# Placing a batch's exponentials behind every chunk of layers 1 to 3, and stretching the pacing sum from 1150 to 1195

## The chip, the cores and the metric

The kernel runs on one core of a Trainium2 chip. The metric is the device time of one execution in microseconds (us). Five executions of the kernel before gave 10002.39, 10005.69, 10021.45, 10026.64 and 10043.83 us, so the median is 10021.45 us.

## The reference, cut to what matters

The input x is (4, 64, 64, 128) in float32: four independent batches of 4096 tokens with 128 channels. Four layers follow one another, each with residual additions.

```python
# layer 0: deformable attention. 4 groups g of 32 channels, 9 sampled points, 4 bilinear corners
qkv = depthwise3x3(gn(x) @ w_qkv + b_qkv) + b_dw
off[g] = conv1x1(pconv(q, pconv_off_w[g]), w_off[g]);  mask = sigmoid(conv1x1(pconv(q, ...)))
ks, vs = bilinear samples of k and v at 9 moved points, times mask     # a gather by data
attn = softmax(q . ks over the 9 points)
x = x + (sum(attn * vs) @ w_proj + b_proj)
# layer 1: linear attention (softmax of q over channels, of k over tokens), then a norm
x = x + norm(linear_attention(gn(x)))
# layer 2: t = t + q * sum(k * v); then 64 experts, each picks its 8 best tokens
t = t + q * (k * v).sum(tokens)
pooled = top-8 tokens of each expert, weighted by the router's softmax over the tokens
t = t + scatter(gelu(pooled @ w1[e] + b1) @ w2[e] + b2)
# layer 3: causal linear attention, then 16 spectral filters (long causal convolutions)
t = t + causal_linear_attention(ln(t))
t = t + sum_k (filter_k * u) @ M_k (plus and minus) + autoregressive part   # u = ln(t)
```

## The kernel before, in words

**Two streams.** The kernel is written as one program in which the function `hybrid` interleaves two streams. While layer 0's attention of batch b runs, layers 1 to 3 of batch b - 1 run beside it; beside batch 0 the tables of the filters are prepared instead (`prepare`, with its own pacing sum `SETUP`). The last batch's layers 1 to 3 have nothing beside them and run at the end with more buffers (`wide`).

**Layer 0's attention.** A batch has 8 chunks c, each with 4 tiles t of 128 tokens, each with 4 groups g: 128 groups. `Layer0.attend` (L591) issues one group and then yields. A group is nine indirect gathers on POOL into the tile gt (L604), each of 128 rows; VectorE's products and sums pr, s, s times weights, sc and mx (L613 to L623); one exponential ex on ScalarE (L626), which is two instructions in the trace; then VectorE's qa (L630), pv (L635) and o (L638). gt has three buffers, so that the gathers of a group wait for pv of the third group before it; pr and pv have one buffer each. Beside it `front(b + 1)` computes layer 0's projections for the next batch during the first 15 of the batch's 32 tiles.

**Layers 1 to 3.** `Post.run` is a generator called `behind`. It yields after each small step, and gives with the yield a number that stands for the step's time. In order: layer 1; layer 2's attention; the router (8 chunks, then the pooling of the chosen tokens), the experts in 16 steps of four experts, the scatter in 8 steps; layer 3's attention; the tokens and the autoregressive part; the filters' front, 128 filter cycles of 4.7 each, and an end stage of 20. An expert step loads its weights on SyncE's queue (w1 and w2, three buffers each), multiplies on PE into ph (L1106), copies hs on ScalarE, transposes on PE into pt (L1115), adds a bias on VectorE (g, L1120), applies Gelu on ScalarE and multiplies on PE into po (L1126). A filter cycle is `convolve` (eight matmuls, 16 in the trace, from the table th and the spectrum xh into pq, L1397, and two copies y on ScalarE, L1411) and `mix` (eight matmuls, 16 in the trace, from the cycle before's y into pa, L1422); `put` writes four finished rows. The words "the end stage" and "layer 0's last rows" in what follows mean the last 20 units of the filters and `end`, which projects a chunk and writes it out.

**Pacing.** After each group `hybrid` takes steps from `behind` until their numbers sum to `total * (groups done) / 128`, where total is `WORK` = 1150. The steps taken after one group are called that group's chunk here. The numbers of layers 1 to 3 sum to 1209.6 before the change and after it, so that with 1150 some steps are left when the 128 groups are issued; they follow the last group, before the next batch's first.

**Order on each engine.** The program's order isn't the order on the engines. A scheduler places each instruction on its engine by the time at which it expects its inputs, and instructions of the two streams overtake each other. `tc.issue_after(ins)` fixes one such relation: what is issued within it stands behind `ins` on its engine. The class `Turns` keeps such marks. Before the change, an exponential stands behind the last copy y of the filters' cycles issued so far (`after("filters")`), and a copy y stands behind the last exponential issued so far (`after("samples")`). The mark "filters" is removed at the end of each batch, so that in layers 1 to 3 ahead of the filters only the scheduler decides.

Of the kernel before, what the change touches and what calls it, by code (L numbers as in the profile page):

```python
# [56 lines left out]
class Turns:  # L57


    def __init__(self, tc):  # L60
        self.tc = tc
        self.last = {}

    def after(self, who):

        ins = self.last.get(who)
        return nullcontext() if ins is None else self.tc.issue_after(ins)

    def took(self, who):
        self.last[who] = next(  # L70
            i for i in reversed(self.tc.nc.cur_bb.bb.instructions)
            if i.engine == mybir.EngineType.Activation
        )


def make_consts(tc, ctx):
# [97 lines left out]
class Layer0:  # L174
# [416 lines left out]
    def attend(self, b, c, t):  # L591

        nc = self.nc
        blk = self.blk[b, c]
        o = blk.o

        qa = blk.qa[t // 2]
        q0 = t % 2 * C
        den = self.sm.tile([P, G], F32, tag="den", name="den")
        for g in range(G):  # L600
            gt = self.gp.tile([P, K2, 256], F32, tag="gt", name="gt")
            for i in range(K2):
                col = g * K2 + i
                nc.gpsimd.indirect_dma_start(  # L604
                    out=gt[:, i, :], out_offset=None, in_=self.tbl[b % 2][:, :],
                    in_offset=bass.IndirectOffsetOnAxis(
                        ap=blk.idx[:, t, col : col + 1], axis=0
                    ),
                )
            corners = gt.rearrange("p i (c s) -> p (i c) s", c=4)  # L610
            cw = blk.cw[:, t, g * K2 : (g + 1) * K2, :]
            pr = self.t1.tile([P, 4 * K2, 32], F32, tag="pr", name="pr")
            nc.vector.tensor_mul(  # L613
                pr, corners[:, :, 0:32],
                qa[:, q0 + 32 * g : q0 + 32 * g + 32].unsqueeze(1).to_broadcast([P, 4 * K2, 32]),
            )
            s4 = self.sm.tile([P, 4 * K2], F32, tag="s4", name="s4")
            nc.vector.tensor_reduce(s4, pr, AX.X, ALU.add)  # L618
            nc.vector.tensor_mul(s4, s4, cw.rearrange("p i c -> p (i c)"))
            sc = self.sm.tile([P, K2], F32, tag="sc", name="sc")  # L620
            nc.vector.tensor_reduce(sc, s4.rearrange("p (i c) -> p i c", c=4), AX.X, ALU.add)
            mx = self.sm.tile([P, 1], F32, tag="mx", name="mx")
            nc.vector.tensor_reduce(mx, sc, AX.X, ALU.max, negate=True)  # L623
            ex = self.sm.tile([P, K2], F32, tag="ex", name="ex")
            with self.turns.after("filters"):
                nc.scalar.activation(ex, sc, AF.Exp, bias=mx, accum_out=den[:, g : g + 1])  # L626
            self.turns.took("samples")
            a0 = 2 * C + g % 2 * 4 * K2
            aw = qa[:, a0 : a0 + 4 * K2]
            nc.vector.tensor_mul(  # L630
                aw.rearrange("p (i c) -> p i c", c=4), cw,
                ex.unsqueeze(2).to_broadcast([P, K2, 4]),
            )
            pv = self.t1.tile([P, 4 * K2, 32], F32, tag="pv", name="pv")
            nc.vector.tensor_mul(  # L635
                pv, corners[:, :, 32:64], aw.unsqueeze(2).to_broadcast([P, 4 * K2, 32]),
            )
            nc.vector.tensor_reduce(  # L638
                o[:, t, 32 * g : 32 * g + 32], pv.rearrange("p i s -> p s i"), AX.X, ALU.add
            )  # L640
            if g < G - 1:
                yield
        nc.vector.reciprocal(den, den)
        og = o[:, t, :].rearrange("p (g c) -> p g c", g=G)
        nc.vector.tensor_mul(og, og, den.unsqueeze(2).to_broadcast([P, G, 32]))
        yield
# [41 lines left out]
class Post:  # L688


    def __init__(self, tc, k, a, pool, dram):
        self.tc, self.nc, self.k, self.a, self.wp = tc, tc.nc, k, a, pool
        self.u = [dram.tile([N, C], F32, name=f"u{i}") for i in range(2)]
        self.x = [dram.tile([N, C], F32, name=f"x{i}") for i in range(2)]
        self.ln = dram.tile([N, C], F32, name="ln")
        self.oe = dram.tile([E, C], F32, name="oe")
        self.fd = dram.tile([2, NB, W * C], F32, name="fd")
        self.yd = dram.tile([NQ, 2, P, C], F32, name="yd")
        self.wide = False
        self.ws = self.mm = None  # L700

    def pool(self, ctx, name, bufs, space=None):
# [82 lines left out]
    def run(self, b, x1, stu, out):  # L785

        with ExitStack() as ctx:
            self.ws = self.pool(ctx, "fwx", 10) if self.wide else None
            sm = self.sm = self.pool(ctx, "psm", 1)
            self.norm = [Norm(self.nc, self.k, sm, NT, f"n{i}") for i in range(2)]  # L790
            xa, xb = x1[b], self.x[b % 2]
            yield from self.layer1(xa, xb)
            yield from self.layer2_attn(xb, xa)
            yield from self.layer2_ffn(xa, xb)
            yield from self.layer3_attn(xb, xa)
            yield from self.stu_tokens(stu, xa, self.u[b % 2], xb)
        yield from self.stu_filters(stu, self.u[b % 2], xb, out[b])
# [512 lines left out]
    def stu_filters(self, s, ud, xd, out):  # L1310
# [40 lines left out]
        with ExitStack() as ctx:  # L1351
# [39 lines left out]
            def convolve(xh, t, q):  # L1391

                pq = ps_q.tile([P, 2, 2, 2, 2, TCOLS // 2], F32, tag="p", name="pq")
                for pair in range(2):
                    for r in range(4):
                        rows = slice(32 * r, 32 * r + 32)
                        nc.tensor.matmul(  # L1397
                            pq[:, r // 2, r % 2, :, pair, :],
                            lhsT=xh[rows, 2 * (q % 4) + pair, :],
                            rhs=t[rows, 2 * (q % 2) + pair, :].rearrange("p (l x) -> p l x", l=2),  # L1400
                            start=True, stop=True,
                        )
                y = yp.tile([P, 4, 2, TCOLS], F32, tag="y", name="y")
                for par in range(2):
                    to = y[:, 1:3] if par else y[:, 0:4:3]
                    src = pq[:, :, par].rearrange("p f l a x -> p l f (a x)")
                    if par and self.wide:
                        nc.vector.tensor_copy(to, src)  # L1408
                    else:
                        with self.turns.after("samples"):  # L1410
                            nc.scalar.copy(to, src)  # L1411
                        self.turns.took("filters")
                return y

            def mix(pa, y, kc, h):
# [291 lines left out]


STEPS = 4 + 1 + 8 + 8
WORK = 1150.0  # L1710
SETUP = 250.0


def hybrid(tc, a, out):
# [3 lines left out]
    with ExitStack() as ctx:  # L1718
# [13 lines left out]
        with ExitStack() as l0ctx:  # L1732
            l0 = Layer0(tc, k, a, x1, d, l0ctx)
            post.mm = l0.mm
            post.turns = l0.turns = Turns(tc)
            front = l0.front(0)
            for _ in range(STEPS - 8 + 2):
                next(front)
# [4 lines left out]
            for b in range(B):  # L1743
# [3 lines left out]
                for c in range(8):  # L1747
                    ahead = (b, c + 1) if c < 7 else (b + 1, 0) if b + 1 < B else None
                    l0.begin(b, c)
                    for t in range(4):  # L1750
                        slot = 4 * c + t
                        if t == 0:

                            if slot == 0 and b == 0:
                                for _ in front:
                                    pass
                            if ahead:
                                l0.where_from(*ahead)
                            l0.query(b, c, 1)
                        elif t == 2 and ahead:  # L1760
                            l0.query(*ahead, 0)
                        for g, _ in enumerate(l0.attend(b, c, t)):
                            while spent < total * (4 * slot + g + 1) / 128:
                                spent += next(behind, total)
                        if t == 0 and last:
                            l0.end(*last)
                            last = None
                        if t == 2 and ahead:
                            l0.where(*ahead)
                        if b + 1 < B:  # L1770
                            if slot == 0:
                                front = l0.front(b + 1)
                                steps = 0
                            while steps < STEPS and steps < STEPS * (slot + 1) / 14:
                                next(front)
                                steps += 1
                            if slot == 14:
                                for _ in front:
                                    pass
# [7 lines left out]
                        last = None  # L1787
                for _ in behind:
                    pass
                post.turns.last.pop("filters", None)  # L1790
        post.mm = None
        post.wide = True
        for _ in post.run(B - 1, x1, stu, out):
# [36 lines left out]
```

## Time and profile before

| | before |
|---|---|
| median of 5 executions | 10021.45 us (10002.39 to 10043.83) |
| the profiled execution's own time | 10016.86 us |
| its span | 10015.1 us |
| mean granted clock of PE | 0.755 of full speed |
| exponentials of batches 0 / 1 / 2 / 3, last one ends | 1942 / 4163 / 6441 / 8678 us |
| last batch's rest, with no groups beside it | 8678 to 10015 us |
| longest wait between two exponentials of a batch, in batches 1 / 2 / 3 | 71.6 / 104.8 / 143.9 us |

The three long stretches, some 2220 to 2280 us each, are one batch's layer 0 beside the preceding batch's layers 1 to 3. The longest waits all come before exponential 66 of the batch, where the first filter copies are. The busy shares of the engines in the profile are averages over these stretches, which have different limits inside; the times of a stretch's stages are told by the first and last instruction of each tile. "remote" as the releaser of a wait, or "another core or an unknown queue" in the chain, is a wait whose end the profile can't put down to a recorded instruction. The lines are those of the kernel before; the change moves later ones by a few.

### The profile page before, as it was taken

How to read it: one execution, taken by the hardware profiler on the slowest of the kernel's cores; microseconds unless marked ns; L12 is line 12 of the kernel's file. 1: busy time of each engine (PE TensorE's matmuls, PEld its weight loads, DVE VectorE, ACT ScalarE, POOL GpSimd, SP SyncE). 2: the span in 40 equal slices, each digit the busy share in tenths (PEclk: the TensorE clock that was granted, in tenths of full speed). 3: DMA queues.
4: the chain of work that ended last, by engine and by line, in shares of the span. 5: the costliest groups of instructions: out<-in, count | busy, mean ns of one | idle time of the engine just before them, and what ended most of it. 6: DMA issues, size and time to landing. Idle time of an engine off the chain costs nothing.

```text
span 10015.1 us, 86749 instructions
## 1 busy us (share of the span) xinstructions
PE 5955.2 (59%) x30155; PEld 4142.3 (41%) x30155; DVE 4626.2 (46%) x7777; ACT 2243.7 (22%) x4156; POOL 4410.0 (44%) x4736
## 2 busy tenths in 40 slices
PE   7455100056666776556666776654446776757899
PEld 6242000034344555435334554422224554535676
DVE  1555555475464444456454443457453444343222
ACT  3100000023122222222222222212222222242222
POOL 0666666654543555555442554555542555200000
PEclk9677555567787888778777888765667888867999
DMA  6444333334644444445554444454543444524322
GB/s 210 138 125 115 105 101 102 100 110 138 191 146 134 118 118 114 110 131 145 179 157 120 122 120 110 108 136 126 177 147 109 120 114 109 145 78 130 105 69 80
DMA packets 1130831, 1255.00 MB, mean 125 GB/s; under 512 B 392478, under 2 KB 923161, under 8 KB 1126169
## 3 DMA queue, kind: packets, MB, share of 16 engines
q1 hardware_dynamic: 906797, 644.20, 23.7%
q0 software_dynamic: 221184, 604.27, 21.3%
q8 instruction: 239, 3.92, 0.2%
q14 instruction: 199, 1.63, 0.1%
q10 hardware_dynamic: 2412, 0.98, 0.0%
HBM read 1061.76 MB, written 187.22 MB: 125 GB/s over the span
## 4 chain that ended last, share of the span: by engine, by line
PE 22%; another core or an unknown queue 12%; ACT 5%; issue 5%; DVE 4%; DMA 3%; SPq 0%; POOL 0%; DVEq 0%; ACTq 0%
PE pa L1422 10%; PE pq L1397 4%; ACT y L1411 2%; DMA xin<-x 1%; PE po L1301 1%; PE ph L1106 1%; DVE o L638 0%; ACT ln L142 0%; PE pt L721 0%; PE pt L1115 0%; PE po L1126 0%; PE pa L1217 0%; DMA yc<-yd 0%; DVE ln_st L125 0%
## 5 line engine op out<-in xcount | busy, mean ns | idle before, releaser
L604 POOL DMA_INDIRECT gt<-tbl,idx x4608 | 4401.0, 955 | 4196.7 <-DVE pv L635 2316.3
L1422 PE MATMUL pa<-y,m 128*128 128x256 f32 x8192 | 2168.7, 417 | 271.1 <-issue 207.0
L1422 PEld LDWEIGHTS pa<-y,m 128*128 128x128 f32 x8192 | 1659.1, 208 | 773.8 <-issue 476.9
L1411 ACT COPY y<-pq 128x1024 f32<-128x1024 f32 x896 | 869.3, 1015 | 2381.9 <-remote 1497.4
L630 DVE TENSOR_TENSOR qa<-cw,ex 128x36 f32<-128x36 f32 x512 | 104.0, 203 | 2431.9 <-ACT ex L626 2300.2
L1397 PE MATMUL pq<-th,xh 32*128 32x256 f32 x8192 | 721.8, 460 | 713.2 <-ACT y L1411 505.8
L638 DVE TENSOR_REDUCE o<-pv 128x32 f32<-128x1152 f32 x512 | 1076.4, 2102 | 12.5 <-remote 6.9
L613 DVE TENSOR_TENSOR pr<-gt,qa 128x1152 f32<-128x1152 f32 x512 | 689.8, 1347 | 310.8 <-DMA gt<-tbl,idx 222.1
L1397 PEld LDWEIGHTS pq<-th,xh 32*128 32x128 f32 x8192 | 438.4, 213 | 926.5 <-ACT y L1411 559.6
L422 PE MATMUL pm<-wd,xT 128*128 128x256 f32 x2376 | 628.5, 416 | 226.6 <-ACT kv L433 122.3
L635 DVE TENSOR_TENSOR pv<-gt,qa 128x1152 f32<-128x1152 f32 x512 | 691.5, 1351 | 41.8 <-remote 15.7
L618 DVE TENSOR_REDUCE s<-pr 128x36 f32<-128x1152 f32 x512 | 687.1, 1342 | 1.7 <-DVE qm L866 1.0
L422 PEld LDWEIGHTS pm<-wd,xT 128*128 128x128 f32 x2376 | 486.2, 210 | 337.2 <-ACT kv L433 142.1
L626 ACT ACTIVATE ex<-sc,mx 128x9 f32<-128x9 f32 x512 | 157.1, 307 | 1197.4 <-DVE mx L623 421.9
L455 PE MATMUL pm<-xT,wd 128*128 128x512 f32 x576 | 303.8, 670 | 148.2 <-ACT qo L472 88.7
L1408 DVE COPY y<-pq 128x1024 f32<-128x1024 f32 x128 | 156.7, 1224 | 466.2 <-ACT y L1411 466.2
L573 PE MATMUL qa<-sident,qt 128*128 128x128 f32 x256 | 52.7, 336 | 440.7 <-issue 291.3
L1106 PE MATMUL ph<-w,pooled 128*1 128x512 f32 x512 | 234.1, 784 | 70.1 <-DMA w<-in_L_ffn_weight_dram 51.6
L1120 DVE TENSOR_TENSOR g<-pt,b1T 128x16 f32<-128x16 f32 x64 | 11.2, 175 | 509.9 <-PE pt L1115 412.2
L455 PEld LDWEIGHTS pm<-xT,wd 128*128 128x128 f32 x576 | 114.3, 212 | 313.6 <-issue 178.4
L142 ACT ACTIVATE ln<-xin,ln,ln 128x128 f32<-128x128 f32 x512 | 211.0, 482 | 132.8 <-DMA xin<-x 116.5
L654 PE MATMUL pt<-ident,o 128*128 128x128 f32 x128 | 33.3, 345 | 344.8 <-issue 153.8
(373 smaller groups left out, 6376.7 us busy)
## 6 DMA issues: line engine op xcount, KB each, us to landing
w<-in_L_ffn_weight_dram SPq DMA_DIRECT2D x512, 256.0 KB
th<-th SPq DMA_DIRECT2D x512, 256.0 KB
gt<-tbl,idx POOLq DMA_INDIRECT x4608
xin<-x SPq DMA_DIRECT2D x256, 256.0 KB
x<-xin SPq DMA_DIRECT2D x160, 256.0 KB
tbl<-kv SPq DMA_DIRECT2D x264, 128.0 KB
th<-wx SPq DMA_DIRECT2D x32, 1024.0 KB
q<-qd SPq DMA_DIRECT2D x288, 64.0 KB
```

The costliest lines, as they stand in the source:

```text
L142: self.nc.scalar.activation(dst, src, AF.Identity, bias=self.shift[:, i : i + 1], scale=self.rstd[:, i : i + 1])
L422: nc.tensor.matmul(pm[:, t, :], lhsT=self.xf[:, at : at + P], rhs=self.wd[:, tap, C:], start=(t == 0 and tap == 0), stop=False,)
L455: nc.tensor.matmul(pv, lhsT=self.wd[:, tap, :C], rhs=self.xT[:, 8 * c + dy : 8 * c + dy + 8, dx : dx + HW], start=(tap == 0), stop=False,)
L604: nc.gpsimd.indirect_dma_start(out=gt[:, i, :], out_offset=None, in_=self.tbl[b % 2][:, :], in_offset=bass.IndirectOffsetOnAxis(ap=blk.idx ...
L613: nc.vector.tensor_mul(pr, corners[:, :, 0:32], qa[:, q0 + 32 * g : q0 + 32 * g + 32].unsqueeze(1).to_broadcast([P, 4 * K2, 32]),)
L618: nc.vector.tensor_reduce(s4, pr, AX.X, ALU.add)
L635: nc.vector.tensor_mul(pv, corners[:, :, 32:64], aw.unsqueeze(2).to_broadcast([P, 4 * K2, 32]),)
L638: nc.vector.tensor_reduce(o[:, t, 32 * g : 32 * g + 32], pv.rearrange("p i s -> p s i"), AX.X, ALU.add)
L1106: nc.tensor.matmul(ph[32 * j : 32 * j + 1, :], lhsT=pooled[:, 16 * j + q : 16 * j + q + 1], rhs=w1s[j], start=True, stop=True,)
L1397: nc.tensor.matmul(pq[:, r // 2, r % 2, :, pair, :], lhsT=xh[rows, 2 * (q % 4) + pair, :], rhs=t[rows, 2 * (q % 2) + pair, :].rearrange("p ...
L1411: nc.scalar.copy(to, src)
L1422: nc.tensor.matmul(pa[:, h * 2 * P : (h + 1) * 2 * P].rearrange("p (g x) -> p g x", g=8), lhsT=s.m[u][:, KC * kc + i, :], rhs=yv[:, i], st ...
```

## The change

The exponentials' mark is taken from all of layers 1 to 3. `mark()` notes how many instructions the program has; `took(who)` looks for the last ScalarE instruction issued since the mark, and keeps the old mark where there is none. In `hybrid`, after a group's chunk, `took("behind")` marks the chunk's last ScalarE instruction, and the next group's exponential is issued behind it. This begins where `Post.run` sets `paced`, that is with batch 1's groups; the last batch's layers 1 to 3 have no groups beside them. The filters' copies y stand behind the last exponential as before; copies of other steps of layers 1 to 3 have no such mark. The mark isn't removed at a batch's end any more. `WORK` goes from 1150 to 1195, so that each group's chunk is 9.34 units instead of 8.98, and 14.6 units instead of 59.6 are left behind the last group.

```diff
 class Turns:
     def __init__(self, tc):
         self.tc = tc
         self.last = {}
+        self.seen = 0
...
+    def mark(self):
+        self.seen = len(self.tc.nc.cur_bb.bb.instructions)
+
     def took(self, who):
-        self.last[who] = next(
-            i for i in reversed(self.tc.nc.cur_bb.bb.instructions)
-            if i.engine == mybir.EngineType.Activation
-        )
+
+        for i in reversed(self.tc.nc.cur_bb.bb.instructions[self.seen :]):
+            if i.engine == mybir.EngineType.Activation:
+                self.last[who] = i
+                break
...
-            with self.turns.after("filters"):
+            with self.turns.after("behind"):
+                self.turns.mark()
                 nc.scalar.activation(ex, sc, AF.Exp, bias=mx, accum_out=den[:, g : g + 1])
             self.turns.took("samples")
...
-        self.wide = False
+        self.wide = self.paced = False
...
             xa, xb = x1[b], self.x[b % 2]
+            self.paced = True
             yield from self.layer1(xa, xb)
...
                         with self.turns.after("samples"):
                             nc.scalar.copy(to, src)
-                        self.turns.took("filters")
...
-WORK = 1150.0
+WORK = 1195.0
...
-            post.turns = l0.turns = Turns(tc)
+            turns = post.turns = l0.turns = Turns(tc)
...
                         for g, _ in enumerate(l0.attend(b, c, t)):
+                            turns.mark()
                             while spent < total * (4 * slot + g + 1) / 128:
                                 spent += next(behind, total)
+                            if post.paced:
+                                turns.took("behind")
...
                 for _ in behind:
                     pass
-                post.turns.last.pop("filters", None)
```

## The prediction

> **What bounds it now.** I read the page first (busy shares, then the costliest groups), then the waits, then busy time by stage, then one stretch of the timeline.
>
> ```profile
> span 10015.1 us, 86749 instructions
> PE 5955.2 (59%) x30155; PEld 4142.3 (41%) x30155; DVE 4626.2 (46%) x7777; ACT 2243.7 (22%) x4156; POOL 4410.0 (44%) x4736
> L604 POOL DMA_INDIRECT gt<-tbl,idx x4608 | 4401.0, 955 | 4196.7 <-DVE pv L635 2316.3
> L1411 ACT COPY y<-pq 128x1024 f32<-128x1024 f32 x896 | 869.3, 1015 | 2381.9 <-remote 1497.4
> ```
>
> No engine is full, and ScalarE, which the change reorders, is the emptiest. So this is a kernel of waits.
>
> Busy time by stage (start and end, length, then busy time and instructions of PE, PEld, DVE, ACT, POOL, then PE's granted clock) shows batch 2's five stages: its lead, layer 1 to the router, the experts, the scatter to the filters' start, the filters. The rows from 8777 on are the last batch's layers 1 to 3, which run with no groups beside them.
>
> ```profile
> 4163.00:4366.00 203.00, 96.26 (x430) 61.99 (x431) 101.90 (x144) 30.31 (x60) 113.19 (x120) 0.69 0.50 134
> 4366.00:4850.00 484.00, 315.59 (x1365) 238.37 (x1363) 299.43 (x608) 144.31 (x341) 237.88 (x244) 0.81 0.49 136
> 4850.00:5136.00 286.00, 164.44 (x889) 65.29 (x889) 113.33 (x160) 56.21 (x102) 136.21 (x145) 0.71 0.62 191
> 5136.00:5449.00 313.00, 211.61 (x972) 152.72 (x972) 161.85 (x379) 82.25 (x169) 93.65 (x100) 0.80 0.44 128
> 5449.00:6441.00 992.00, 691.57 (x3867) 512.00 (x3865) 425.65 (x579) 263.27 (x397) 517.94 (x547) 0.82 0.46 115
> 8678.00:8740.00 62.00, 56.14 (x370) 44.14 (x368) 3.96 (x5) 22.77 (x26) 0.00 (x0) 0.98 0.83 231
> 8777.00:9024.00 247.00, 148.52 (x593) 101.23 (x595) 117.31 (x325) 102.31 (x221) 0.00 (x0) 0.64 0.25 75
> 9024.00:9128.00 104.00, 78.67 (x768) 38.68 (x768) 3.30 (x17) 17.61 (x38) 0.00 (x0) 0.70 0.74 224
> 9128.00:9356.00 228.00, 156.94 (x796) 125.43 (x796) 90.03 (x255) 66.59 (x132) 0.00 (x0) 0.81 0.30 97
> 9356.00:9975.00 619.00, 615.65 (x4157) 481.33 (x4158) 156.69 (x128) 147.67 (x159) 0.00 (x0) 0.99 0.28 69
> ```
>
> The same stages counted by tile ex (each exponential is two ScalarE instructions) give 14, 28, 16, 10 and 61.5 groups in batch 2. Layers 1 to 3 alone need 247, 104, 228 and 619 us for the last four stages. The difference, shared over the groups that ran beside, is what a group costs them: (484 - 247)/28 = 8.5 us, (286 - 104)/16 = 11.4, with three early filter cycles (619/128 = 4.84 us each) taken off (313 - 228 - 14.5)/10 = 7.0, and (992 - 115.5 x 4.84)/61.5 = 7.0; the lead, with its ten cycles and 40 us of end stage, (203 - 48 - 40)/14 = 8.2. Batch 1 (603, 300, 317, 1001 us with 36, 18, 14, 61.5 groups) gives 9.9, 10.9, 5.7, 7.1; batch 3 (199, 466, 281, 307, 984 us with 13.5, 29, 16, 9, 61) gives 8.2, 7.6, 11.1, 7.7, 6.9. So each batch's time is the work of layers 1 to 3 plus 6 to 11 us for every group. Why so much shows here:
>
> ```profile
> 3422.33 1.15 PE L1397 MATMUL pq<-th,xh 32*128 32x256 f32 x16 [1.53 <-issue]
> ...
> 3434.46 0.95 POOL L604 DMA_INDIRECT gt<-tbl,idx  x1 [0.30 <-issue]
> 3437.70 1.01 ACT L1411 COPY y<-pq 128x1024 f32<-128x1024 f32 x1 [15.14 <-remote]
> ```
>
> The matmuls that the copy reads are recorded as done at 3423.5, yet the copy starts at 3437.7, some 2 us after the group's ninth gather. The page books 1497.4 us of such waits before L1411 alone. Nine gathers at 1.25 us are 11.3 us per group, about the price found above. A group takes time from layers 1 to 3 mainly through its gathers, wherever ScalarE's order puts its exponential; that governs the sum.
>
> **The change, part by part.** From the order in which the built kernels list each engine's instructions.
>
> *Where the groups lie.* Before, 118 of 128 cycles are copied before batch 1's last exponential; ten follow among the next batch's first eight groups. After, all 128 are, in each batch, and the next layer 1's first copies stand after exponential 1 of the batch, not 13. The 16 expert steps, spread over 14 to 15 exponentials, come two at a time between exponentials 33 and 42. A batch's 128 groups are then 33 (lead and layer 1 to router), 9 (experts), 21 and 65.
>
> Own work: 247 + 104 + 228 + 128 x 4.84 = 1199 us. Groups: 33 x 9.9 = 327 (batch 1's rate, the one batch that starts layer 1 without a lead, as all now do; bounds 7.6 and 10.3, the latter a group's VectorE chain from ex to the next mx, uncovered); 9 x 11.1 = 100 (low bound; high if the experts stay at 286: 182); 21 x 6.8 = 143 (5.7 to 10.3); 65 x 7.0 = 455. Together 1025, so 2224 us for batch 1; batches 2 and 3 also carry three quarters of the end stage's 40 us, 2254 each: 6732. Before, 1942 to 8678 is 6736. This part is -4 us: ten cycles come into batch 1 (+48), groups leave the dear experts.
>
> *The tail.* The ten cycles after the last group stood 62 us (8678 to 8740) with nothing beside; now the last mix and its output remain, about 10 us by the kernel's very end (last copy 9967, last oT 9976). -52.
>
> Here the Trainium skill speaks against it: TensorE: Matmul & The Clock Gate, Part 1, says PE drops to half rate after an idle window of about 3.4 us and is full only after a busy one. The rows agree: granted clock 0.98 in that tail, 0.82 in the filters beside groups. By that rule, 4.84 x 0.99/0.82 makes each moved cycle 1 us dearer, +10 us in all as an estimate; the cycle cost beside groups above already holds it.
>
> *The stall.* Before, the first filter copy made exponential 66 wait: from 5340 to 5449 one exponential ran, none from 3090 to 3162, one from 7550 to 7694. It looks like 320 us to gain, but layers 1 to 3 ran alone there at their own speed; the groups that would fill it bring their gathers. I count 0; were half hidden, -160.
>
> *Function tables.* LoadActFuncSet falls from 133 to 117: 16 x 1.28 us (ACT_TABLE_LOAD rows) = 20; half on the path, -10.
>
> *New waits.* An exponential now stands behind the last ScalarE instruction of its chunk. Behind it VectorE's qa, pv and o wait, POOL's next gathers wait for pv, and VectorE's later work of layers 1 to 3 stands after qa. Against that, ScalarE now idles before L626 for 108.5, 45.6 and 94.9 us in the three batches' first four stages, the chunk's copies queued behind; exponentials that come later wait less. I set the two off: 0, bounds -125 and +200.
>
> *Nothing else moves in amount*: SP's loads and POOL's gathers are as many; took's search and the removed pop issue nothing.
>
> Sum: -4 - 52 - 10 = -66 on the profiled execution's 10016.86 (span 10015.1 and 1.8 around it), 9951; that execution lies 4.6 us under the median 10021.45: 9955.
>
> **Rivals.** About 30 us, 0.3%, is what a measurement of this kernel can tell from no change.
>
> *Slower: the group's own chain becomes the bound.* From exponential to next mx VectorE needs 10.3 us; if the chunk's VectorE steps stand behind qa, chunk and chain alternate. Experts: two steps per exponential, each passing PE, ScalarE, VectorE and PE; they may keep 286 us with 9 groups instead of 16, for three weight buffers against the tail's ten: +82 per batch. C: 21 x 3.5 = +74 more. It decides from 0.4 us per group outside the filters on (3 x 54 x 0.4 = 65). With half of both, +234: 10190; a third, 10110. For: VectorE waits 139.7 us for g in batch 1, and POOL's 2316.3 behind pv. Against: in the filters, already in such an order, 16.2 us per group hold 1.9 cycles, 9.2 us alone, and not 19.5.
>
> *No change*: moved groups cost alike everywhere (8.4), the boundary twice shows batch 1's extra, 10020. For: the rates differ more by batch than by stage outside the experts.
>
> *More*: ScalarE's idle before exponentials goes by half (-125) and layer 1 runs at batch 2's rate: 9820. For: the filters' 7.0 under a fixed order is the lowest steady rate. Against: the filters have long PE stretches, layer 1 many short hand-overs.
>
> **Numbers.** Forecast 0.36, slower chain 0.36, no change 0.14, more 0.14. The likeliest by a hair is 9955; its own range 9900 to 9990. Over all: 9790 (the "more" case with a little of the stall) to 10130 (a third of the slow case and some). Faster 0.50, same 0.14, slower 0.36.
>
> **What would show it.** Right: filters near 1075 to 1085 us per batch with 65 groups; experts near 205 us; no gap of 70 to 144 us between exponentials; after the last exponential under 20 us to the end stage; ScalarE's idle before L626 in layers 1 to 3 down, VectorE's before qa up. Wrong if experts stay above 250 us with 9 groups, if groups outside the filters cost over 10 us, or if batches 2 and 3 start with a gap beyond 60 us while layer 1 waits for layer 0's last rows.

## The result, and the profile after

The changed kernel takes 9972.76 us (median of 27 executions, 9933.94 to 10014.69), the kernel before in the same comparison 10013.09 us (48 executions): a ratio of 0.9959, 95% interval 0.9949 to 0.9968, or 40 us faster. The prediction said 9955.0 us, 66 us faster on its own base. In the profiled executions the span went from 10015.1 to 9974.9 us, so these two traces show the same 40 us.

The page of the changed kernel, the lines that answer to those shown of before (costliest groups: busy time and mean ns, then the idle time ahead and what ended it):

```profile
span 9974.9 us, 86687 instructions
PE 5972.8 (60%) x30155; PEld 4113.4 (41%) x30155; DVE 4630.5 (46%) x7777; ACT 2226.3 (22%) x4140; POOL 4418.3 (44%) x4736
L609 POOL DMA_INDIRECT gt<-tbl,idx x4608 | 4409.4, 957 | 4201.2 <-DVE pv L641 2484.8
L1418 ACT COPY y<-pq 128x1024 f32<-128x1024 f32 x896 | 869.3, 1014 | 2496.2 <-remote 1483.9
```

The busy shares are what they were. ScalarE has 16 instructions fewer, the function tables. The copies y still wait 1483.9 us (1497.4 before) for something that the profile can't name. So the kernel is bound as before, and the time has to be found in the stages.

Busy time by stage, columns as in the prediction: batch 2's layer 1 to the router, experts, scatter to the filters' start, filters; then the end stage of batch 3's filters and the last batch's four stages alone:

```profile
4300.00:4794.00 494.00, 293.96 (x1180) 215.07 (x1179) 314.96 (x608) 144.69 (x335) 257.05 (x263) 0.73 0.46 128
4794.00:5057.00 263.00, 190.16 (x1048) 85.47 (x1046) 86.06 (x138) 51.18 (x96) 96.97 (x103) 0.86 0.66 200
5057.00:5441.00 384.00, 214.04 (x922) 151.53 (x922) 232.10 (x476) 81.64 (x186) 184.33 (x193) 0.73 0.45 134
5441.00:6520.00 1079.00, 778.98 (x4267) 556.97 (x4268) 447.49 (x605) 290.68 (x433) 546.43 (x576) 0.82 0.44 113
8678.00:8724.00 46.00, 28.34 (x79) 14.72 (x77) 9.25 (x12) 2.46 (x6) 0.00 (x0) 0.81 0.72 199
8724.00:8982.00 258.00, 143.22 (x596) 96.42 (x599) 118.50 (x329) 102.12 (x221) 0.00 (x0) 0.67 0.36 110
8982.00:9085.00 103.00, 76.62 (x768) 35.72 (x760) 3.50 (x18) 17.74 (x38) 0.00 (x0) 0.77 0.75 227
9085.00:9318.00 233.00, 160.92 (x812) 128.01 (x812) 89.95 (x254) 66.65 (x132) 0.00 (x0) 0.80 0.31 98
9318.00:9927.00 609.00, 606.64 (x4111) 473.99 (x4110) 155.51 (x127) 146.20 (x158) 0.00 (x0) 0.99 0.28 68
```

POOL's counts, divided by nine, give the groups: 29, 11, 21 and 64. The 62 us with ten filter cycles after the last exponential have gone: what follows it is the last mix and the end stage, 46 us instead of 95.

The two spans differ by three terms. The first exponential of batch 1 is 4.2 us earlier. From there to the last exponential of batch 3 it is 6739.4 us instead of 6735.0, so +4.4. From there to the end it is 1297.2 instead of 1337.6, so -40.4. **The whole gain lies behind the last exponential.** The new order moved groups between stages over 6700 us and left the sum where it was.

### The profile page after: what moved, and what is told of

Its sections match the earlier page's. It is cut to its first block, busy times and chain, and to the rows that moved or that the text cites. A ratio compares the mean times of both kernels' runs of the same rounds, so it can differ in the third digit from the quotient of the medians.

```text
span 9974.9 us, 86687 instructions
## 1 busy us (share of the span) xinstructions
PE 5972.8 (60%) x30155; PEld 4113.4 (41%) x30155; DVE 4630.5 (46%) x7777; ACT 2226.3 (22%) x4140; POOL 4418.3 (44%) x4736
## 4 chain that ended last, share of the span: by engine, by line
PE 33%; another core or an unknown queue 26%; issue 12%; DVE 11%; ACT 8%; DMA 5%; POOL 3%; SPq 1%; DVEq 0%; ACTq 0%; POOLq 0%
PE pa L1428 12%; PE pq L1404 5%; ACT y L1418 4%; POOL gt L609 3%; PE pm L427 3%; DVE o L644 2%; PE pm L460 1%; DMA xin<-x 1%; DVE s L623 1%; DVE pr L618 1%; PE ph L1113 1%; DVE pv L641 1%; PE pq L861 1%; PE pm L502 1%
## 5 line engine op out<-in xcount | busy, mean ns | idle before, releaser
L1428 PEld LDWEIGHTS pa<-y,m 128*128 128x128 f32 x8192 | 1635.0, 205 | 865.1 <-issue 636.3
L1418 ACT COPY y<-pq 128x1024 f32<-128x1024 f32 x896 | 869.3, 1014 | 2496.2 <-remote 1483.9
L502 PE MATMUL pm<-q,weff 128*81 128x512 f32 x192 | 150.2, 930 | 264.1 <-ACT xr L670 112.6
L578 PEld LDWEIGHTS qa<-sident,qt 128*128 128x128 f32 x256 | 43.3, 231 | 471.2 <-issue 302.2
```

The lines of the kernel that those rows point to most:

```text
L502: nc.tensor.matmul(pm[:NOFF, :].rearrange("p (t r x) -> p t r x", t=4, r=2), lhsT=self.weff[:, i, :], rhs=q3[:, i].rearrange("p (r t) x -> ...
L1428: nc.tensor.matmul(pa[:, h * 2 * P : (h + 1) * 2 * P].rearrange("p (g x) -> p g x", g=8), lhsT=s.m[u][:, KC * kc + i, :], rhs=yv[:, i], st ...
```

## The experiments

The first four kernels shared one chip, the second four another, the last four a third. Each ratio is against the kernel before on the same chip; its medians there were 9912.97, 9925.65 and 7895.75 us. How the third differs is told further down; times of that chip are not set beside those of the other two. Between the first two, ratios are compared, and these carry over only roughly: the changed kernel itself has 0.9959 above and 0.9918 on the second chip, with intervals that don't meet. Times in the first four expectations are on the base of 10013 us. The wait of an exponential is told here from the start of the one before it to its own start; in this measure exponential 66 of the kernel before waits 84, 128 and 165 us, where the table ahead of the prediction counts only from the end of the mx that it reads.

### WORK alone

```diff
 # the kernel before
-WORK = 1150.0
+WORK = 1195.0
```

> The kernel before with WORK at 1195 and nothing else. Theory A (the gain is the tail's, and WORK makes it): the last exponential stays near 8680 us, the filter cycles left behind it fall from ten to one or none, and the time falls by about 40 us to 9970 to 9985. Theory B (the order of the exponentials makes the gain): the scheduler still lets the exponentials of layers 1 to 3 run ahead, the cycles still spill over the batch's end, and the time stays within 10 us of before, 10005 to 10025.

Measured: 9853.42 us, ratio 0.9944 (0.9930 to 0.9959), 60 us less by the medians. In its trace (of its fastest execution, 9806.37 us) the last exponential is at 8514.6 and the last matmuls into pq begin at 8512.3: no cycle is left behind. Theory A's reason holds, with a gain somewhat over its 40 us; its 8680 us for the last exponential belongs to the result's base. So the rest of the change isn't needed for the gain. Its trace also bears on a point of the prediction: exponential 63 of the batches still waits 103, 112 and 105 us before the filters, the stall that looked like 320 us to be won. The kernel with the stall is as fast as one without it on the same chip (the open boundary below, 9846.08 us).

### The order alone

```diff
 # the changed kernel
-WORK = 1195.0
+WORK = 1150.0
```

> The changed kernel with WORK back at 1150. Theory A: the tail has its 9 or 10 filter cycles again after the last exponential and costs what it did, 40 us more than the changed kernel; the three batches in sum take what they take in the changed kernel; 10005 to 10025. Theory B: nearly all of the gain stays, 9970 to 9985.

Measured: 9959.24 us, ratio 1.0049 (1.0030 to 1.0068): **slower than before by 46 us**, which neither theory expected. ScalarE at the start of batch 2, first in the changed kernel, then in this one (start, length, line, operation, and in brackets the idle time ahead):

```profile
4244.71 0.31 ACT L632 ACTIVATE ex<-sc,mx 128x9 f32<-128x9 f32 x1
...
4300.07 0.59 ACT L404 COPY xT<-pt 128x512 f32<-128x512 f32 x1 [28.22 <-PE pt L403]
...
4304.99 0.59 ACT L829 COPY xT<-pt 128x512 f32<-128x512 f32 x1 [1.29 <-PE pt L828]
4306.15 0.59 ACT L829 COPY xT<-pt 128x512 f32<-128x512 f32 x1 [0.57 <-PE pt L828]
4306.63 0.31 ACT L632 ACTIVATE ex<-sc,mx 128x9 f32<-128x9 f32 x1
```

```profile
4179.68 0.32 ACT L632 ACTIVATE ex<-sc,mx 128x9 f32<-128x9 f32 x1
...
4212.04 1.93 ACT L1418 COPY y<-pq 128x1024 f32<-128x1024 f32 x2 [2.80 <-PE pq L1404]
4216.77 1.93 ACT L1418 COPY y<-pq 128x1024 f32<-128x1024 f32 x2 [2.80 <-PE pq L1404]
...
4280.22 1.08 ACT L829 COPY xT<-pt 128x512 f32<-128x512 f32 x2
4282.86 0.59 ACT L829 COPY xT<-pt 128x512 f32<-128x512 f32 x1 [1.56 <-PE pt L828]
4283.34 0.31 ACT L632 ACTIVATE ex<-sc,mx 128x9 f32<-128x9 f32 x1
```

L829 is layer 1's first copy of the next batch. Exponential 1 stands behind it in both. In the changed kernel that is a wait of 61.9 us in batch 2 and 59.8 in batch 3. With 1150 the eight filter cycles left over, 4.7 us each, run first and alone, and the waits are 103.7 and 92.8 us. In the kernel before, such leftovers ran beside the next batch's first eight groups. Set against the changed kernel run again (below; waits of 60.4 and 59.7 us, 1290.8 us from the last exponential to the end, median 9849.04), exponential 1's two waits are 196.5 - 120.1 = 76 us longer, and the tail, 1335.6 us, is 45 us longer: 121 of the 144 us by which the two profiled executions differ (9994.4 and 9850.7; the medians differ by 110). The two ran on different chips. That the boundary's wait itself makes the 76 us is an inference from these traces, which a later run did not confirm.

### The boundary opened

```diff
 # the changed kernel
-                            if post.paced:
+                            if post.paced and slot > 0:
                                 turns.took("behind")
...
                 for _ in behind:
                     pass
+                turns.last.pop("behind", None)
```

> The changed kernel, with the mark removed at a batch's end and none taken after the batch's first four groups. In the changed kernel exponential 1 of batches 2 and 3 waits 61.9 and 59.8 us, behind layer 1's first copies, while layer 0's last rows go out to memory and come back. Theory A, first reading (a group beside working layers costs them 7 to 11 us, a group in that gap costs nothing): three or four groups move into the gap of each of three boundaries, 3 x 3 x 8 = 72 us less, 9900 to 9935, and no wait over 40 us before exponential 1. Rival: the gap's groups hold up the end stage and layer 1's start by as much as they save later: 9965 to 9980.

Measured: 9846.08 us, ratio 0.9924 (0.9904 to 0.9943). Exponential 1 of batches 2 and 3 no longer waits over 33 us, but exponential 5, the first that has a mark again, waits 66.9 and 68.2 us. The gap has moved by four groups and is as long as it was. The ratio lies at the edge of what theory A expected (0.989 to 0.992 on its base), but the changed kernel had not been run on this chip; on the second it has 0.9918 and a median 3 us away, so the 72 us that I expected are not there.

### The experts' exponentials left to the scheduler

```diff
 # the changed kernel, layer2_ffn
+                self.paced = False
                 for q in range(16):
...
+                self.paced = True
                 nc.sync.dma_start(oe, self.oe[:, :])
```

> The changed kernel, with no new marks taken during the 16 expert steps, so that the scheduler places the exponentials there as before. Theory A (a group costs 11 us among the experts and 7 in the filters): the experts hold 14 to 16 groups again and 270 to 300 us instead of 190 to 205, the filters lose 5 or 6 groups and 40 us; 3 x 30 = 90 us more, 10040 to 10070. Rival (a group costs the same everywhere): within 15 us of the changed kernel, 9960 to 9990, with the same shift of groups.

Measured: 9900.98 us, ratio 0.9988 (0.9972 to 1.0004), 55 us above the open boundary on the same chip. Against the changed kernel's two ratios that is 29 or 69 us more, between the two expectations. Theory A's reason is wrong: from the first ph matmul to the last g the experts hold as many groups as in the changed kernel (8, 8 and 10), and not 14 to 16. They are placed otherwise: exponential 41, the next with a mark, waits 106.7, 104.5 and 66.3 us, and the stage takes 253, 244 and 222 us; with marks it was 237, 237 and 197 on the same chip (the run before this one, from the first ph to the last g as here). One group at a time beside every second expert step costs less than the same groups in a bunch and a wait.

### The changed kernel again

> The changed kernel itself, on the chip of the next three runs. So far WORK alone gave 0.9944 of before, the order alone 1.0049, the changed kernel 0.9959. Theory A': WORK makes the gain by emptying the tail, and the order costs about 15 us of it: 0.995 to 0.997. Rival: the order helps where little is left at the batch's end, and the changed kernel is at or below WORK alone: 0.992 to 0.9945.

Measured: 9849.04 us, ratio 0.9918 (0.9892 to 0.9944). That is below the range of theory A' and a hair below the rival's. It overlaps WORK alone (0.9930 to 0.9959), but from another chip; and in the result the same kernel had 0.9959, above WORK alone's 0.9944. On one chip, WORK alone and the order with the open boundary are 7 us apart (9853.42 and 9846.08). So the 15 us that theory A' laid on the order aren't seen, nor is a gain by it shown: with 14.6 units left at the batch's end, the order is worth nothing that these runs can tell, within some 0.3%.

### WORK at 1240

```diff
 # the kernel before
-WORK = 1150.0
+WORK = 1240.0
```

> The kernel before with WORK at 1240, so that all 1209.6 units, the filters' end stage too, are issued by group 125 of 128. Theory A' (what stands behind the last exponential is what counts): the end stage's 44 us of the last batch come beside the last groups and the gain over before grows by 20 to 40 us: ratio 0.990 to 0.9925. Rival (the last three groups then run with nothing beside them, 13 us each in each batch, and give it back): 0.994 to 0.997.

Measured: 9817.03 us, ratio 0.9899 (0.9871 to 0.9926), on the chip of the run above and 32 us below the changed kernel there. From the last exponential to the end it is 1260 us now: the end stage's last additions come 22 us after that exponential, not 46 to 48. The 31 us that this stretch lost account for the difference. **This one number in the kernel before gives the lowest ratio of the versions on these two chips**; its interval overlaps the changed kernel's.

### One gather per group, and one wide gather

```diff
 # the changed kernel; first: 256 floats of the first point, which serve all nine
-            for i in range(K2):
-                col = g * K2 + i
-                nc.gpsimd.indirect_dma_start(
-                    out=gt[:, i, :],
...
-                        ap=blk.idx[:, t, col : col + 1], axis=0
+            nc.gpsimd.indirect_dma_start(
+                out=gt[:, 0, :],
...
+                    ap=blk.idx[:, t, g * K2 : g * K2 + 1], axis=0
 # second: 2304 floats in one piece, as many bytes as nine gathers
+            nc.gpsimd.indirect_dma_start(
+                out=gt.rearrange("p i c -> p (i c)"),
...
+                    ap=blk.idx[:, t, g * K2 : g * K2 + 1], axis=0
```

> The changed kernel with one gather of 128 x 256 floats per group in place of nine; its values serve all nine points, so that VectorE's work keeps its size and the output is another. Theory A (a group takes its 7 to 11 us from layers 1 to 3 through its nine gathers, which hold back PE's completion signals): the filters' stage with 64 groups falls from 1053 to 1084 us to 650 to 750, layer 1 to the router with 30 to 33 groups from 463 to 563 to 300 to 400, the ScalarE copies' unexplained waits before L1418 fall from 1484 to under 300 us. Rival (a group's cost is its VectorE and ScalarE steps between those of layers 1 to 3): the filters stay above 950 us.

> The changed kernel with one gather per group that fetches the same bytes in one piece, 128 rows of 2304 floats for 9 x 128 rows of 256 (other rows, so another output). If the gathers' instructions and descriptors on POOL are the price, it runs like the kernel with one small gather. If the bytes are, it runs like the changed kernel: filters above 1000 us. Theory A expects the first.

Measured: 7074.88 and 7285.23 us (one execution each; before on this chip 9888.35 to 9954.95). Both kernels leave out most of the points that the nine gathers fetch. Against the changed kernel's 9849.04 there, one small gather takes 2774 us off, and one wide one, with as many bytes, still 2564. Theory A came true in both, with the filters' stage at 645 and 642 us, a little under its range. The wider rows cost 210 us. The wide gather has fewer instructions, fewer rows and neighbouring addresses at once; which of the three makes the difference wasn't separated. ScalarE's longest waits (who waited for what; total, times, longest) in the result's trace of the changed kernel, then with one small gather, then with one wide one:

```profile
ACT y L1418 <- remote: 1483.9, 151, 20.5
ACT y L1418 <- PE pq L1404: 895.1, 318, 16.8
```

```profile
ACT y L1421 <- PE pq L1407: 1183.1, 473, 15.4
ACT ex L634 <- DVE mx L630: 910.0, 185, 11.4
```

```profile
ACT y L1416 <- PE pq L1402: 1200.1, 488, 13.4
ACT ex L630 <- DVE mx L626: 946.7, 202, 11.1
```

"remote" is gone, and the copies wait for the matmuls that they read. For each PE instruction that signals, the trace also has the time from its recorded end to the semaphore's next update. In the changed kernel 34% of those within a run of gathers or 2.5 us after it come more than 3 us late (mean 4.34 us, 1405 instructions); away from gathers 1% do (mean 0.01). With one small gather it is 4% (mean 0.15), with one wide one 2% (mean 0.07). An update up to half a microsecond ahead of the recorded end is counted as the instruction's own; with another bound the shares shift by two or three points. Whether the matmul's data are late too, or its signal alone, these traces don't tell. The Trainium skill, Perfetto Trace Analysis, section Tensor Engine Instruction, says that PE's end is computed and that the update follows PSUM's acknowledgement; the trace agrees that the recorded end and the signal are two events, and shows by how far they can part.

What a group costs the stages, from xt's last addition to the first ph, to the last g, to the first pq, to the last pq, less the same stage of the last batch alone (252, 96, 235, 611 us), divided by the groups of batch 2:

| us per group | layer 1 to router | experts | scatter to filters | filters |
|---|---|---|---|---|
| changed kernel again, nine gathers | 7.8 (32) | 17.6 (8) | 7.2 (22) | 6.8 (64) |
| one gather | 4.2 (32) | 10.2 (8) | 2.4 (22) | 0.5 (64) |
| nine gathers on the third chip (WORK at 1240, below) | 5.0 (30) | 10.5 (8) | 2.8 (22) | 1.2 (62) |

In the filters nearly all of the price was the gathers'. Among the experts more than half stays: there a group's VectorE steps may alternate with those of the expert step; this wasn't tried.

### The boundary open, with WORK at 1150

The edits of the open boundary, with WORK = 1150.0; third chip.

> The order of the changed kernel with the open boundary (no mark across a batch's end, none from the batch's first four groups) and WORK at 1150. The order alone at 1150 ran at 1.0049 of before, 46 us slower, and its exponential 1 waited 104 and 93 us in batches 2 and 3. Theory C (the order costs nothing except at the batch's end, where the steps left over hold exponential 1 and the groups behind it): most of the 46 us come back, ratio 0.998 to 1.002. Rival (the order costs time inside the layers at this pacing): it stays at 1.003 to 1.006.

Measured: 8002.45 us, ratio 1.0141 (1.0125 to 1.0156), outside both ranges: exponential 5 waits 112.5 and 115.2 us while the filter cycles that are left over run alone. As at 1195, the opening only moves the wait. Theory C's remedy fails; whether its cause is right this run can't say, since it did not remove the wait.

### The changed kernel with 1240, and with the boundary open too

> The changed kernel with WORK at 1240. The kernel before with 1240 gave 0.9899. Theory A' (the order is worth nothing where little is left at the batch's end; what WORK takes off the tail is what counts): 0.988 to 0.992, within 20 us of WORK alone at 1240. Rival (the marks hold the last groups' exponentials behind the end stage, which passes through memory twice, and exponential 1 behind layer 1's first copies): 0.994 to 0.998.

> The changed kernel with the open boundary and WORK at 1240. Theory A': 0.987 to 0.992, no more than 15 us from the changed kernel with 1240. Rival (the boundary's gap of 60 us is worth its groups): 0.983 to 0.987.

Measured: 7850.71 us, ratio 0.9943 (0.9930 to 0.9957), and 7840.71 us, ratio 0.9926 (0.9913 to 0.9940). The first lies in the rival's range and outside theory A's; the second lies between the two ranges, 10 us from the first, within the 15 us that theory A' allowed. The ranges came from the other two chips, so the miss of the first doesn't show that the marks cost time: with no steps left over, exponential 1 waits only 24 and 25 us. Both kernels are faster than before; WORK at 1240 without the order was not run on this chip.

### No marks

```diff
 # the kernel before, WORK = 1195.0
-            with self.turns.after("filters"):
-                nc.scalar.activation(ex, ...)
+            nc.scalar.activation(ex, ...)
```

> The kernel before with WORK at 1195 and no mark for the exponentials anywhere, in the filters neither; the copies y stand behind the exponentials as before. Theory D (a group's price is its nine gathers, wherever its exponential is placed): within 25 us of WORK alone, 0.992 to 0.997. Rival (the filters' fixed order is worth something of itself): the filters' stage grows by over 40 us per batch, 1.005 or more.

Measured: 8406.45 us, ratio 1.0646 (1.0631 to 1.0660): the rival's case. The filters' order is worth a lot on this chip: without it most exponentials have one cycle between them, not two; others wait up to 139 us while bunches of 9 to 27 cycles run; 23 cycles are left for after the batch's last exponential; and batch 2's filters, from the first pq to the last, take 905 us, against 686 with marks at 1240. This chip shows none of the late signals that go with the price elsewhere, so theory D stays untested where they occur.

### The third chip

The same program with the same gathers takes 7895.75 us there, some 20% less. Waits of ScalarE in the changed kernel with WORK at 1240 on that chip, and the page's line of its gathers:

```profile
ACT ex L632 <- DVE mx L628: 1913.0, 267, 19.6
ACT y L1418 <- PE pq L1404: 1104.5, 462, 16.6
```

```profile
L609 POOL DMA_INDIRECT gt<-tbl,idx x4608 | 4402.6, 955 | 2132.7 <-issue 1329.4
```

A gather takes 955 ns as elsewhere, but there are no unexplained waits before y, and of 1836 PE signals in or just after gathers none is more than 3 us late. Batch 2's filters with 62 groups take 686 us, 1.2 us per group over the 611 alone, and in every stage of the table above nine gathers here cost little more than one gather does on the second chip. So what a group takes from layers 1 to 3 on the other two chips goes with the late signals and not with the gathers' time as such, unless these chips differ in something else that the traces don't show. What the gathers still cost here is their own issue: batch 0's 128 groups take 1444 us, 11.4 each, and nine gathers at 1.25 us are 11.25; with one gather on the second chip they take 960. What makes one chip hold the signals back and another not, these runs don't show.

## Why the prediction was right, point by point

**What bounds the kernel: right, and the base of the rest.** "A group takes time from layers 1 to 3 mainly through its gathers, wherever ScalarE's order puts its exponential". The one-gather and wide-gather kernels show the first half. It holds for over nine tenths of the price in the filters, for two thirds in the scatter, for about half in layer 1, and for some 40% among the experts. The second half holds only roughly: the orders tried on the first two chips at 1195 lie within 55 us of one another, the order at 1150 is 46 us slower than before, and the order without marks on the third chip costs 6%.

**The stall at exponential 66 counted at 0: right.** WORK alone keeps it at 103 to 112 us and has the full gain. That fits the prediction's reason, that layers 1 to 3 use this time at their own speed.

**The tail, -52: right in its place, 12 too large.** From the last exponential to the end stage's last addition it went from 94.7 to 46.3 us, so -48.4. The last batch's layers then took 8.0 us longer (1238.6 to 1246.6), 6 of them in layer 1 to the router; no cause was looked for.

**The batches, -4, and the function tables, -10: +4.4 together.** Stage by stage the working was worse than its sum:

| us, batches 1 / 2 / 3 | predicted | measured |
|---|---|---|
| lead and layer 1 to router | 574 / 604 / 604 | 555 / 557 / 523 |
| experts | 204 | 267 / 263 / 212 |
| scatter to filters | 371 | 388 / 384 / 371 |
| filters to the last exponential | 1075 | 1089 / 1079 / 1052 |
| sum | 2224 / 2254 / 2254 | 2299 / 2283 / 2158 |

The failed step is "9 x 11.1 = 100" for the experts, by one price per group. By the exponentials, 12, 12 and 11.5 groups lay in the table's stage instead of 9, at 13.6, 13.3 and 9.4 us each. The table's windows reach 13 to 26 us beyond the expert steps; from the first ph to the last g there were 8, 8 and 10 groups instead of 16, 14 and 15, and the time went only from 277, 264 and 255 to 241, 238 and 199 us. So batches 1 and 2 kept some 90% of the stage's time with little over half of its groups: the price went up as the groups went out. That is what the first half of the rival *the group's own chain* said, and the signs "experts stay above 250 us" and "over 10 us" for a group outside the filters came true there. It cost 130 us over the three batches. The other failed step paid for it: "33 x 9.9", batch 1's price laid on all batches. In sum layer 1 was 147 us under the forecast, 81 of them in batch 3. That batch alone has no next batch's front beside it, which may be why its first stages came cheaper; it wasn't tried, and in the kernel before the same stages of batch 3 were only 22 us below batch 2's. Two errors of that size that cancel are luck, not skill: the total was better founded than the parts.

**New waits, set at 0 with bounds -125 and +200: about right in size, for another reason.** VectorE's idle before qa in the first four stages went down, from 118.9, 149.0 and 153.8 to 99.3, 75.9 and 80.2 us, where the prediction said up. ScalarE's before the exponential, over the same windows, went from 108.5, 107.9 and 161.1 to 108.6, 99.0 and 98.6; the prediction's 45.6 and 94.9 leave the lead out. The wait that did come was at the boundary, 61.9 and 59.8 us, at the edge of the sign that the prediction named at "beyond 60 us". At 1195 it costs nothing that shows in the comparison with WORK alone; at 1150 the same marks made kernels that are slower than before, on two chips (1.0049 and, with the boundary open, 1.0141). The prediction priced the two edits by terms of one sum; by these runs the order is safe only where WORK empties the batch's end.

**Two figures of the rivals.** From the exponential to the next mx the prediction gave VectorE 10.3 us. Its instructions of that stretch (qa, pv, o, pr, s twice, sc, mx) take 0.20 + 1.35 + 2.10 + 1.35 + 1.34 + 0.19 + 0.19 + 0.16 = 6.9 us on average in the trace of before. No row shows the rest, so the upper bound of layer 1's price and the chain of the rival were set too long. And 9820 for the case *more* has the 125 us of its first half and almost nothing for its second: 33 groups at 8.4 instead of 9.9 us would be another 50 us per batch. Neither enters the forecast.

**The clock.** The prediction drew on the Trainium skill, TensorE: Matmul & The Clock Gate, Part 1, which has PE at half rate after an idle window. The traces agree in direction: with one gather and 64 groups beside them, batch 2's filters ran at a granted clock of 0.99, with PE busy for 641 of 645 us; with nine gathers at 0.82, busy for 779 of 1079 (the row further up). The row with one gather:

```profile
3624.00:4269.00 645.00, 641.45 (x4274) 495.98 (x4275) 446.40 (x600) 292.07 (x431) 60.47 (x64) 0.99 0.37 87
```

## What to carry to other kernels

Where two streams share the engines and their sum of work is fixed, look first at the stretches in which one stream runs alone; here one pacing number moved the last cycles out of such a stretch and made the gain, while reordering ScalarE moved hundreds of us between stages and nothing in total that these runs can tell. Don't count a visible stall as gain until you know what the other stream earns in it. And an order that pins one stream behind the other must be tried with what is left over at its boundaries: the same marks gave level at one pacing and a loss at another.

## What the runs showed of the hardware

- By the trace, PE's completion signals can come late while POOL issues gathers: in 34% of cases by over 3 us after the recorded end, against 1% away from them. Nine gathers of 128 x 1 KB cost this kernel 2564 us more than one of 128 x 9 KB with as many bytes, though one such POOL instruction takes as long for either (957 and 966 ns). Not all of that is late signals: the kernel before on the third chip, without them, still takes 610 us more than the wide gather on the second.
- Whether this happens differed with the chip: the kernel before took 9912.97, 9925.65 and 7895.75 us on three of them, with late signals on the first two alone (and in both traces of the result). Gathers (951 to 958 ns) and exponentials (some 305 ns) have the same durations on all, so these don't tell the chips apart; the unexplained waits do.
